# A second PSUM place for attention scores, a larger share of TensorE for early experts, and a new pace in the tail

## The chip, the cores and the metric

The kernel runs on one core of one Trainium2 chip. TensorE multiplies matrices, VectorE (DVE in the profile), ScalarE (ACT) and GpSimd (POOL) work on vectors, and SyncE (SP) issues most transfers. [...] The metric is the device time of one execution in microseconds. Before the change three executions took 15310.87 us at the median (15308.61 to 15326.58).

## The reference

Two layers work on x of 4 images, 3072 tokens each, 256 features, all in fp32.

Layer 0 is group normalization, a Mamba block along one axis, another along the other axis, and a residual. Layer 1 is attention and then experts:

```python
h = tanh(q[:, :, None, :] + k[:, None, :, :] + bh)     # additive attention, 32 hidden units
e = einsum('biju,u->bij', h, Wa[:, 0]) + ba[0]
v = einsum('bij,bjd->bid', softmax(e), inputs)
...
e = leaky_relu(a_src[src] + a_dst[dst])                # graph attention over 1048576 edges
...                                                    # gates of 4 experts, the best 2 kept
out += g * (gelu(x @ W1[e] + b1[e]) @ W2[e] + b2[e])
```

So every pair of tokens of an image needs 32 tanh values. The gates come from sums over edges: edges are sorted, the table rows of sources and destinations are gathered, and their weighted values are added up by destination. The output of an expert doesn't depend on its gate, so it can be computed before the gates are known and kept in HBM. This kernel does so.

## The kernel before, in words

One program holds everything, and its authors wrote the order of the instructions of TensorE, ScalarE, VectorE and GpSimd out by hand: Python generators yield in turn, and what is called first stands first in each engine's queue. [...]

**Layer 0 with attention beside it** (class Layer0, class Attention). Attention of image b runs while Layer0 works on the following images. When Layer0 has ended, attention of the last image is left. The change acts there and in what follows.

**The last attention** (Attention.units, L776). A unit is 32 queries against all 3072 keys. It takes eight tanh instructions on ScalarE, each 128x3072 (th, L815), and each is followed two iterations later by its scores on TensorE: eight products (16 records in the profile, as each fp32 product shows as two) into the PSUM tile pe (L788). pe is 128 x 2 x 512 fp32. There is one place for it (PE_BUFS = 1). After the eighth scores VectorE takes the maximum of each row (nb, L877), and ScalarE the exponentials (pr, L884), both from pe. Then pr is transposed (ptw, L891), copied (pT, L893) and multiplied with the values (pv, L900). The next unit's first scores overwrite pe, so they wait for pr. In the kernel before they are held back over one yield, so that other TensorE work stands ahead of them:

```python
if k == 0:
    pe = self.ps_e.tile([P, 2, JB], F32, tag="pe", name="pe")
    held = behind.pop(0)
else:
    scores(pe, k, behind.pop(0))
```

**Work beside it** (steps, in whole, L1966). Each call of units advances steps once for VectorE and once for TensorE. VectorE's part is the sorting of edges (Edges.sort): compaction with many element-wise instructions, and then one-hot rows (L1219) whose products count edges on TensorE (L1233). For TensorE there is a credit us_t: each th adds SLOT_US and takes off what the attention's own steps need (0.7, 0.4 and 2.9 us a unit, and 1.8 for every fourth). A group of one-hot products costs 8 x PRODUCT_US; what is left goes to early experts.

**Early experts** (Experts.early, L1644). A unit is here a block of 512 tokens with one expert. Its hidden layer is eight products of 128x512 into ph (L1632), two for each of four results, taken out by VectorE with the bias (L1671). Two units then share one visit of ScalarE for GELU (L1676), which needs a table load there and back. The outputs (L1640, into po) are taken out by VectorE (L1683) and kept in HBM. ph has two banks in this phase, po one. 22 units are done so; others were done beside layer 0; 37 are left.

**The tail** (tail, L1730). It counts in steps, three to a remaining expert unit. Each unit computes hidden results, GELU on ScalarE straight from ph (L1714) and outputs. Between them stand the graph's parts: GpSimd issues 540 indirect gathers of table rows (gs, L1337, and the rest of gd, L1052), 16 for a batch of 12 columns up to the 27th of the 36 batches, 12 for the later ones, at most four batches ahead. VectorE scores a batch and builds one-hot tiles (L1374, L1378), and TensorE adds it up (pa, L1388). Batch m is scored at step G0 + PART*m//2. RATE gathers are credited after each of six points of a unit, and a small instruction of GpSimd (pace, L1047) that reads the tile just made ties them to that point. h1 has two buffers, so GELU of a unit waits for the pace instructions of the unit two before it. When a quarter of the graph is done, its gates follow (finish), and then the kept outputs of its six blocks are fetched, weighted and added (L1717) and stored.

PSUM results of the tail come from two pools each (bank, L1594): one counter is shared by ph and po and its parity chooses the pool.

Of the kernel before, what the change touches and what calls it, by code (L numbers as in the profile page):

```python
# [17 lines left out]
F32 = mybir.dt.float32  # L18
# [6 lines left out]
PSUM = bass.MemoryType.PSUM  # L25

P = 128
# [21 lines left out]
TH_BUFS, PE_BUFS, PV_BUFS = 3, 1, 1  # L49
JB = 512  # L50
# [9 lines left out]
G1, K1 = 8, 4  # L60
GP, GG = 12, 4
EDGE_US = 2.4
FIRST, RATE = 14, 2.75
G0, PART = 10, 6
KO_BUFS = 2
SLOT_US, PRODUCT_US = 1.2, 0.11
EU, EG = 32, 2
TB = 512
NQ, FC, NBLK_X = TB // P, FF // P, M // TB
# [570 lines left out]
class Attention:  # L640
# [4 lines left out]
    def __init__(self, ctx, tc, ident, a, x1, x2, xn2T, tab_s, tab_a):  # L645
        self.nc = nc = tc.nc
        self.ident, self.x1, self.x2, self.xn2T = ident, x1, x2, xn2T
        self.tab_s, self.tab_a = tab_s, tab_a
        pool = lambda name, bufs, **k: ctx.enter_context(
            tc.tile_pool(name=name, bufs=bufs, side="right", **k))  # L650
        const = self.const = pool("atc", 1)
        self.rows, self.th, self.wk = pool("atr", 2), pool("atb", TH_BUFS), pool("atw", 1)
        self.ps_e = pool("ate", PE_BUFS, space=PSUM)
        self.ps_v = pool("atv", PV_BUFS, space=PSUM)

        def load(name, shape, ap):
            t = const.tile(shape, F32, tag=name, name=name)
            nc.sync.dma_start(t, ap)
            return t

        self.wt = load("wt_rep", [P, KC, P], a["wt_rep"].rearrange("(k p) m -> p k m", p=P))
        self.wx = load("wx_rep", [P, KC, P], a["wx_rep"].rearrange("(k p) m -> p k m", p=P))
        self.bh = load("bh_rep", [P, 1], a["bh_rep"])
        self.wa = load("wa_blk", [P, P // (4 * R_ATT), QU], a["wa_blk"])
        self.ba = load("ba_rep", [P, 1], a["ba_rep"])
        self.wg = load("wg", [P, KC, HF], a["W_gat"].rearrange("(k p) f -> p k f", p=P))
        self.asr = load("as_rep", [P, HF], a["as_rep"])
        self.adr = load("ad_rep", [P, HF], a["ad_rep"])
        self.eps = const.tile([P, 1], F32, tag="eps1", name="eps1")
        nc.vector.memset(self.eps, 1e-5)  # L670

        self.sel = const.tile([P, QU], F32, tag="sel", name="sel")
        nc.vector.tensor_tensor(self.sel, ident[:, :QU], ident[:, QU:2 * QU], ALU.add)
        for q in range(2, P // QU):
            nc.vector.tensor_tensor(self.sel, self.sel, ident[:, q * QU:(q + 1) * QU], ALU.add)
        self.state = [{} for _ in range(B)]

        self.krep, self.qsel = ([const.tile([P, n], F32, tag=f"{k}{i}", name=f"{k}{i}") for i in range(2)]
                                for k, n in (("krep", TOK), ("qsel", TOK // R_ATT)))
        self.extra, self.entry, self.col, self.asked, self.normed = 0.0, 0, 0, 0, 0  # L680

        self.later, self.now = [], None
# [93 lines left out]
    def units(self, side):  # L776


        nc = self.nc
        todo, behind = [], []  # L780
        NK = QU // R_ATT
        PER = TOK // R_ATT

        def scores(pe, k, th):
            for j in range(2):
                for q in range(NQT):
                    c0 = q * KQ + j * KQ // 2
                    nc.tensor.matmul(pe[q * QU:(q + 1) * QU, j, :KQ // 2], self.wa[:, k, :],  # L788
                                     th[:, c0:c0 + KQ // 2], start=(k == 0), stop=(k == NK - 1))

        def beside():
            while side:
                try:
                    return next(side[0])
                except StopIteration:
                    side.pop(0)

        i = 0  # L800
        while i < B * PER + LAG or todo or self.later:
            b, col = self.entry, self.col = divmod(i, PER)
            if b < B and "krep" not in self.state[b]:

                yield
                late, self.later = self.later, []
                for f in late:
                    f()
                yield
                beside()  # L810
                continue
            if b < B:
                s = self.state[b]
                th = self.th.tile([P, TOK], F32, tag="th", name="th")
                nc.scalar.activation(th, s["krep"], AF.Tanh, bias=s["qsel"][:, col:col + 1])  # L815
                behind.append(th)
                self.now = th
            else:
                self.now = None
            yield  # L820
            late, self.later = self.later, []
            for f in late:
                f()
            busy = tail = held = None
            if behind and i >= LAG:
                n, k = divmod(i - LAG, NK)
                if k == 0:

                    pe = self.ps_e.tile([P, 2, JB], F32, tag="pe", name="pe")
                    held = behind.pop(0)  # L830
                else:
                    scores(pe, k, behind.pop(0))
                if k == NK - 1:
                    tail = self.unit_tail(*divmod(n, TOK // QU), pe)
                    busy = True

            self.extra = 0.0 if tail or not todo else getattr(todo[0], "us", 0.0)
            yield
            if held:
                scores(pe, 0, held)  # L840
            if tail:

                for f in todo:
                    f()
                todo = tail()
            elif todo and hasattr(todo[0], "us"):
                if not todo[0].full:
                    beside()
                todo.pop(0)()
                busy = True  # L850
            elif todo:
                todo.pop(0)()

            if b < B and col == LAG + 3:
                self.load_values(b)
            if b < B and LAG + 4 <= col < LAG + 10:
                self.normalize_values(b, col - LAG - 4)
            if b and col == LAG + 10:
                side.append(self.after(b - 1, *AFTER[-1]))
            side += [self.after(b, t0, t1) for t0, t1 in AFTER[:-1]  # L860
                     if b < B and col == t1 * P // R_ATT + LAG + 10]
            if busy is None:
                beside()
            i += 1
        side.append(self.after(B - 1, *AFTER[-1]))
# [606 lines left out]
class Beside:  # L1472
# [91 lines left out]
    def bank(self):  # L1564
        return self.l0.ps_x.tile([P, 2, self.half], F32, tag="ex", name="ex")
# [7 lines left out]
class Experts:  # L1573
# [3 lines left out]
    def __init__(self, ctx, tc, x2, xn2T, gates, out, dram, beside=None):  # L1577
        self.nc, self.tc, self.dram = tc.nc, tc, dram
        self.x2, self.xn2T, self.gates, self.out = x2, xn2T, gates, out
        pool = lambda name, bufs, **k: ctx.enter_context(tc.tile_pool(name=name, bufs=bufs, **k))  # L1580
        self.xp, self.hp = pool("fx", 2), pool("fh", 2)
        self.ps_h, self.ps_o = [pool("fp", 2, space=PSUM)], [pool("fo", 1, space=PSUM)]
        self.kept, self.done = (beside.kept, beside.units()) if beside else ({}, [])
        self.xts, self.turn = {}, 0

    def open(self, ctx, w):

        pool = lambda name, bufs, **k: ctx.enter_context(self.tc.tile_pool(name=name, bufs=bufs, **k))
        self.w = w
        self.io = pool("fi", 2)  # L1590
        self.ps_h.append(pool("fp2", 2, space=PSUM))
        self.ps_o.append(pool("fo2", 1, space=PSUM))

    def bank(self, pools, shape, tag):  # L1594
        self.turn += 1
        return pools[self.turn % len(pools)].tile(shape, F32, tag=tag, name=tag)

    @staticmethod
    def weights(pool, nc, a):
# [341 lines left out]
def whole(tc, a, dram, out):  # L1941
# [11 lines left out]
    with ExitStack() as ctx:  # L1953
        actx, lctx, ectx = ExitStack(), ExitStack(), ExitStack()
        with tc.manual_schedule(engines={E.PE, E.Activation, E.DVE, E.Pool}):
# [4 lines left out]
            att = Attention(actx, tc, ident, a, x1, x2, xn2T, tab_s, tab_a)  # L1960
            l0.lead_psum = lambda: att.ps_e.tile([P, 2, JB], F32, tag="pe", name="py")[:, 0, :T]
            l0.beside = Beside(lctx, tc, a, l0, att, xn2T, dram)
            side = []
            late = {}

            def steps():  # L1966

                for done in l0.run():
# [3 lines left out]
                        side.append(att.keys(done))  # L1972
                    yield
                lctx.close()
                keep = ctx.enter_context(tc.tile_pool(name="late", bufs=1))
                late["gates"] = keep.tile([P, NH, NEXP], F32, tag="gates", name="gates")
                ed = late["ed"] = Edges(ctx, tc, a, tab_a)
# [6 lines left out]
                while True:  # L1984
                    us_v = min(us_v, 0.0) + EDGE_US
                    while lists and us_v > 0 and len(ed.todo) < 2:
                        us = next(lists, None)
                        if us is None:
                            lists = None
                            pool = ectx.enter_context(tc.tile_pool(name="late2", bufs=1))  # L1990
# [18 lines left out]
                    yield  # L2009

            flow = steps()
            while not side:
                next(flow)
# [19 lines left out]
        n = most.tile([P, 1], I32, tag="n1", name="n1")  # L2033
# [76 lines left out]
```

## Time and profile before

| What | Value |
|---|---|
| median of three executions | 15310.87 us |
| the profiled execution, its time | 15328.57 us |
| its span, first to last instruction | 15326.8 us |
| TensorE / VectorE / ScalarE / GpSimd busy | 77 / 72 / 79 / 59% |
| transfers of the first edge lists are issued (e, L1135) | 11413.9 us |
| first hidden product of an early expert | 11849.1 us |
| first one-hot product | 12471.5 us |
| last tanh starts | 14201.7 us |
| first GELU of the tail | 14271.4 us |
| last gather | 15164.2 us |
| last scatter product (pa) of the tail | 15244 us |

All times inside a profile count from the first instruction. Busy shares are means over stages that have different limits, so the prediction reads each stage by itself. In lists of waits a line reads: engine and instruction that waited, what ended the wait, total us, times, longest.

### The profile page before, as it was taken

What the parts mean: (1) busy time and instruction counts of PE and PEld (TensorE: products, weight loads), DVE (VectorE), ACT (ScalarE), POOL (GpSimd) and SP (SyncE); (2) the same over time, 40 slices, a digit from 0 to 9 for tenths busy, and PEclk for the clock granted to TensorE, in tenths of its full rate; (3) what the DMA queues carried; (4) which work ended last, traced back from release to release, by engine and by line L of the source; (5) the groups of instructions that cost most, each with busy time, mean ns of one, the idle gap of its engine ahead of it and who ended that gap; (6) DMA issues with size and microseconds to landing.
All of it is one profiled execution on the core that took longest, in us unless ns stands there. A gap on an engine that the chain in (4) does not pass through costs nothing. (4 is left out here: it accounts for less than half of the span.)

```text
span 15326.8 us, 225317 instructions
## 1 busy us (share of the span) xinstructions
PE 11744.9 (77%) x86496; PEld 5137.0 (34%) x86496; DVE 11006.6 (72%) x15895; ACT 12153.9 (79%) x9327; POOL 8997.6 (59%) x6935
## 2 busy tenths in 40 slices
PE   5666764777777767788887777888876778988997
PEld 2222332222222233333333333333332334433554
DVE  7888888777777887777777877577778864321367
ACT  3443334999999979999999899999997889999221
POOL 4555556777777767767767677477750024400684
PEclk8888887888888888989998889999988989999998
DMA  5666665445445444454454444355531000010234
GB/s 192 204 203 200 198 204 167 149 148 156 152 150 151 158 156 148 150 152 151 151 150 156 147 149 152 110 156 151 154 127 37 24 13 13 10 31 22 66 95 138
DMA packets 1209121, 2007.93 MB, mean 131 GB/s; under 512 B 412384, under 2 KB 655712, under 8 KB 1204960
## 3 DMA queue, kind: packets, MB, share of 16 engines
q1 hardware_dynamic: 1180384, 1988.07, 41.6%
q0 software_dynamic: 27648, 5.36, 0.8%
q8 instruction: 680, 11.14, 0.3%
q14 instruction: 409, 3.35, 0.1%
HBM read 1875.19 MB, written 117.83 MB: 130 GB/s over the span
## 5 line engine op out<-in xcount | busy, mean ns | idle before, releaser
L815 ACT ACTIVATE th<-krep,qsel 128x3072 f32<-128x3072 f32 x3072 | 8661.7, 2848 | 411.1 <-PE pe L788 392.0
L788 PE MATMUL pe<-th,wa_blk 128*32 128x384 f32 x49152 | 4999.3, 535 | 1196.7 <-ACT pr L884 957.3
L409 POOL TENSOR_TENSOR h<-h,bC 128x768 f32<-128x768 f32 x2048 | 3756.2, 1834 | 3000.4 <-DVE h L402 2634.4
L402 DVE TENSOR_TENSOR_SCAN h<-dA,dB 128x384 f32<-128x384 f32 x4096 | 3687.3, 942 | 1109.4 <-ACT dA L385 752.9
L788 PEld LDWEIGHTS pe<-th,wa_blk 128*32 128x32 f32 x49152 | 1448.0, 116 | 3775.6 <-issue 1992.1
L393 DVE TENSOR_TENSOR dB<-bB,dtu 128x768 f32<-128x768 f32 x2048 | 1942.3, 948 | 123.3 <-DMA bB<-bc 91.2
L385 ACT ACTIVATE dA<-dt,t_A 128x380 f32<-128x380 f32 x2048 | 1127.1, 571 | 887.6 <-DVE h L402 883.1
L385 ACT ACTIVATE dA<-dt,d_A 128x372 f32<-128x372 f32 x2048 | 1102.9, 562 | 601.3 <-DVE h L402 595.9
L428 PE MATMUL py<-h,ident 128*128 128x384 f32 x2176 | 1010.1, 597 | 679.6 <-POOL h L409 678.2
L416 POOL TENSOR_TENSOR h<-h 128x768 f32<-128x768 f32 x752 | 1423.0, 1892 | 53.6
L900 PE MATMUL pv<-xn,pT 128*32 128x257 f32 x18432 | 1116.1, 391 | 172.3 <-DVE pT L893 171.4
L959 POOL TENSOR_SCALAR sf<-sel,f 128x32 f32<-128x32 f32 x384 | 148.6, 410 | 1641.6 <-ACT f L955 1533.9
L893 DVE COPY pT<-ptw 128x512 f32<-128x512 f32 (+1 forms) x768 | 419.0, 546 | 703.7 <-PE ptw L891 703.0
L428 PEld LDWEIGHTS py<-h,ident 128*128 128x128 f32 x2176 | 445.4, 223 | 1247.6 <-POOL h L409 1015.2
L900 PEld LDWEIGHTS pv<-xn,pT 128*32 128x32 f32 x18432 | 583.5, 112 | 759.7 <-DVE pT L893 317.4
L417 POOL TENSOR_TENSOR h<-h 128x384 f32<-128x384 f32 x752 | 783.7, 1042 | 59.0
L418 POOL TENSOR_TENSOR y<-y,h 128x384 f32<-128x384 f32 x752 | 779.9, 1037 | 59.0
L1714 ACT ACTIVATE h<-ph,b 128x512 f32<-128x512 f32 x148 | 96.7, 685 | 662.9 <-POOL pace L1047 473.9
L1337 POOL DMA_INDIRECT gs<-tab_s,si x432 | 526.6, 1219 | 131.3 <-issue 98.8
L891 PE MATMUL ptw<-ident,pr 128*128 128x128 f32 x2304 | 484.7, 328 | 143.5 <-DVE pT L893 79.6
L902 DVE COPY pvs<-pv 128x257 f32<-128x257 f32 x384 | 160.2, 417 | 569.0 <-PE pv L900 568.8
L1052 POOL DMA_INDIRECT gd<-tab_a,di x432 | 467.2, 1082 | 140.6 <-issue 133.4
(302 smaller groups left out, 15311.0 us busy)
## 6 DMA issues: line engine op xcount, KB each, us to landing
bB<-bc SPq DMA_DIRECT2D x2048, 384.0 KB
bC<-bc SPq DMA_DIRECT2D x2048, 384.0 KB
all<-kept SPq DMA_DIRECT2D x24, 2048.0 KB
x<-x SPq DMA_DIRECT2D x144, 256.0 KB
kept<-ko SPq DMA_DIRECT2D x59, 512.0 KB
x<-x SPq DMA_DIRECT2D x192, 128.0 KB
xt<-xn2T SPq DMA_DIRECT2D x41, 512.0 KB
qsel<-xn2T SPq DMA_DIRECT2D x75, 256.0 KB
```

The costliest lines, as they stand in the source:

```text
L385: nc.scalar.activation(inner(dA[:, :T]), inner(blk["dt"][:, e, :]), AF.Exp, scale=blk["w"]["A"][:, e, i + s:i + s + 1])
L393: nc.vector.tensor_tensor(dB, blk["bB"].pop(j), z["dtu"].unsqueeze(1).to_broadcast([P, SB, T]), ALU.mult)
L402: nc.vector.tensor_tensor_scan(h[:, s, :], z.pop(("dA", e, i + s))[:, :T], z["dB"][:, s, :], 0.0, ALU.mult, ALU.add)
L409: nc.gpsimd.tensor_tensor(h, h, blk["bC"].pop(j), ALU.mult)
L416: nc.gpsimd.tensor_tensor(h0, h0, h1, ALU.add)
L417: nc.gpsimd.tensor_tensor(h0[:, 0, :], h0[:, 0, :], h0[:, 1, :], ALU.add)
L418: nc.gpsimd.tensor_tensor(y[e], y[e], h0[:, 0, :], ALU.add)
L428: nc.tensor.matmul(z["py"], self.ident, h[:, s, :], start=(i == 0), stop=(i == DS - 1))
L788: nc.tensor.matmul(pe[q * QU:(q + 1) * QU, j, :KQ // 2], self.wa[:, k, :], th[:, c0:c0 + KQ // 2], start=(k == 0), stop=(k == NK - 1))
L815: nc.scalar.activation(th, s["krep"], AF.Tanh, bias=s["qsel"][:, col:col + 1])
L900: nc.tensor.matmul(pv[q * QU:(q + 1) * QU, :C + 1], pT[:, i, q * QU:(q + 1) * QU], s["xn"][:, q * NK + i, :], start=(i == 0), stop=(i == N ...
L1337: nc.gpsimd.indirect_dma_start(out=gs[:, u, :], out_offset=None, in_=rows, in_offset=bass.IndirectOffsetOnAxis(ap=ed.si[:, q, c0 + u:c0 + ...
```

## The change

It has four parts.

1. When layer 0 has ended, a second pool with one place for pe is opened. While it is there, the unit's number chooses between the two, by n // NK % 2 (NK is 8), and the first scores are no longer held back over the yield.
2. SLOT_US goes from 1.2 to 1.35.
3. PSUM of the experts: ph has one bank before the tail instead of two, and three more in the tail; ph and po count their turns apart, so that each goes round its banks.
4. In the tail PART goes from 6 to 5 and RATE from 2.75 to 3.2: a batch every 2.5 steps, which is 0.83 units, and 6.4 gathers a step.

```diff
-FIRST, RATE = 14, 2.75
-G0, PART = 10, 6
+FIRST, RATE = 14, 3.2
+G0, PART = 10, 5
 KO_BUFS = 2
-SLOT_US, PRODUCT_US = 1.2, 0.11
+SLOT_US, PRODUCT_US = 1.35, 0.11
...
-        self.ps_e = pool("ate", PE_BUFS, space=PSUM)
+        self.ps_e, self.ps_e2 = pool("ate", PE_BUFS, space=PSUM), None
...
                 n, k = divmod(i - LAG, NK)
                 if k == 0:
-
-                    pe = self.ps_e.tile([P, 2, JB], F32, tag="pe", name="pe")
+                    places = self.ps_e2 if self.ps_e2 and n // NK % 2 else self.ps_e
+                    pe = places.tile([P, 2, JB], F32, tag="pe", name="pe")
+                if k == 0 and not self.ps_e2:
+
                     held = behind.pop(0)
                 else:
                     scores(pe, k, behind.pop(0))
...
-        self.ps_h, self.ps_o = [pool("fp", 2, space=PSUM)], [pool("fo", 1, space=PSUM)]
+        self.ps_h, self.ps_o = [pool("fp", 1, space=PSUM)], [pool("fo", 1, space=PSUM)]
...
-        self.xts, self.turn = {}, 0
+        self.xts, self.turn = {}, {}
...
-        self.ps_h.append(pool("fp2", 2, space=PSUM))
+        self.ps_h += [pool("fp2", 3, space=PSUM)] * 3
...
-        self.turn += 1
-        return pools[self.turn % len(pools)].tile(shape, F32, tag=tag, name=tag)
+        self.turn[tag] = self.turn.get(tag, -1) + 1
+        return pools[self.turn[tag] % len(pools)].tile(shape, F32, tag=tag, name=tag)
...
                 lctx.close()
+                att.ps_e2 = actx.enter_context(
+                    tc.tile_pool(name="ate2", bufs=1, side="right", space=PSUM))
```

## The prediction

> **What bounds the kernel now.** I read the page's 40 slices first, to see where the changed code lies.
>
> ```profile
> PE   5666764777777767788887777888876778988997
> ...
> ACT  3443334999999979999999899999997889999221
> POOL 4555556777777767767767677477750024400684
> ```
>
> The slices up to about the 30th are layer 0 with attention beside it, which the diff leaves alone. In slices 30 to 37 ACT (ScalarE) climbs back to nine tenths: the last attention. Then ACT falls to two and POOL (GpSimd) rises to eight: the tail. Next I asked for busy time by stage: sort alone (A), sort with early experts (B), one-hot products (C), rest of attention (D), tail up to the last gather. Columns: stretch and length, then busy us and instructions of PE, PEld, DVE, ACT, POOL; clock; DMA.
>
> ```profile
> 11425.00:11790.00 365.00, 241.71 (x2212) 100.92 (x2212) 302.49 (x451) 261.19 (x108) 5.74 (x13) 0.83 0.14 40
> 11790.00:12470.00 680.00, 512.24 (x4560) 204.11 (x4560) 604.41 (x998) 554.93 (x230) 21.60 (x24) 0.89 0.08 23
> 12470.00:13620.00 1150.00, 1032.10 (x11017) 489.11 (x11014) 434.95 (x838) 1122.79 (x461) 468.12 (x692) 0.95 0.08 15
> 13620.00:14206.00 586.00, 508.83 (x4845) 215.49 (x4843) 110.46 (x216) 571.45 (x239) 8.20 (x24) 0.95 0.08 25
> ...
> 14245.00:15165.00 920.00, 850.29 (x2530) 492.09 (x2530) 541.14 (x950) 207.93 (x264) 755.74 (x750) 0.96 0.35 91
> ```
>
> In A and B DVE is at 83 and 89%, and ACT idles 28 and 18% of the time. In C and D ACT is at 97.6%. There PE has little to spare: busy 1541 of 1736 us, and the waits (C and D together, engine by engine) fill the rest:
>
> ```profile
> ACT th L815 <- PE pe L788: 35.1, 59, 3.2
> ```
> ```profile
> PE pe L788 <- ACT pr L884: 153.8, 58, 10.7
> ...
> PE pe L788 <- ACT th L815: 10.4, 11, 2.6
> ```
>
> One unit boundary in time, from the timeline, shows what that 153.8 us is:
>
> ```profile
> 12637.55 1.50 PE L788 MATMUL pe<-th,wa_blk 128*32 128x384 f32 x16
> ...
> 12638.98 0.89 PE L1233 MATMUL pc<-hot_go 128*128 128x96 bf16 x8
> 12639.11 0.96 DVE L877 TENSOR_REDUCE nb<-pe 128x1 f32<-128x768 f32 x1 [0.30 <-PE pe L788]
> ...
> 12639.69 1.06 PE L1632 MATMUL ph<-xt,krep 128*128 128x512 f32 x2
> ...
> 12642.15 0.88 ACT L884 ACTIVATE pr<-pe,nb 128x768 f32<-128x768 f32 x1
> ...
> 12643.08 2.79 PE L788 MATMUL pe<-th,wa_blk 128*32 128x384 f32 x16 [2.33 <-ACT pr L884]
> ```
>
> The eighth scores end at 12639.0. DVE needs 0.96 us for the maximum, ACT finishes its tanh (2.08 us more), then pr takes 0.88, and only then may the next scores overwrite pe. PE covers part with a product and a hidden matmul, then waits 2.33 us.
>
> In the tail POOL never stops: 31 gathers and 11 paces per 50 us. ACT waits for it, in units 26.3 us apart on average:
>
> ```profile
> ACT h L1714 <- POOL pace L1047: 465.0, 25, 24.0
> ...
> POOL gs L1337 <- issue: 94.2, 371, 0.4
> ```
> ```profile
> 14394.40 1.27 ACT L1714 ACTIVATE h<-ph,b 128x512 f32<-128x512 f32 x2 [20.91 <-POOL pace L1047]
> ...
> 14421.92 1.27 ACT L1714 ACTIVATE h<-ph,b 128x512 f32<-128x512 f32 x2 [22.12 <-POOL pace L1047]
> ```
>
> From 15025 on ACT waits for PE ph instead and units are 23.4 us apart: there PE is the bound. After the last unit (15213) DVE sets the end.
>
> [...] sixteen score records take 1.50 us, and 2.79 after a 2.33 us wait. [...]
>
> **The change, part by part.**
>
> *Alternating places.* The place is chosen by n // NK % 2, with n the unit's number and NK = 8 th to a unit. It therefore changes every eighth unit, not every unit: at 13 of the 104 boundaries after the second place opens. The other 91 wait for pr as before. Waits for pr were 84.5 us in A (11 times), 72.9 in B (17), 92.5 in C (38), 61.4 in D (20): 7.7, 4.3, 2.4, 3.1 each. Removed: one in A (8 us of PE; I take −5 of time, as DVE at 83% follows), about 2.6 in B (11 us), 9 in C and D (23 us).
>
> *Scores moved ahead.* With a second place, scores of k = 0 are no longer held over the yield. In the instruction order, early-expert and product work between the eighth and the next first scores falls from 1.6 to 1.2 us a unit (priced at 1.0 us a hidden product, 0.48 an output product, 0.9 a group of eight one-hot products), and 0.65 now stands behind the wait. What is queued behind the waiting first scores is PE's whole queue: that work, then ptw. Cover lost: 0.4 us for 19 units in B (8 us) and 62 in C and D (25 us).
>
> *SLOT_US 1.35.* Early units go from 22 to 29, the tail's from 37 to 30. Early and product PE work rises from 112 to 139 us in B, from 269 to 319 in C, from 125 to 154 in D: +27, +50, +29. ACT gets 7 GELUs of 1.90 us and eight more table loads of 1.283: 13.3 + 10.3 = 24 us, nearly all in C and D, where ACT is the bound. Four more GELU visits in C and D make PE wait longer at a boundary: the five long waits there (10.5, 3.0, 4.3, 9.3, 10.7) average 7.6 against 2.3, so 4 × 5.3 = 21 us.
>
> *One hidden bank.* The next hidden product must now wait for DVE's bias add, which stands just ahead of it in the order and behind sort pieces. With two banks the trace shows no such wait, so I bound it: 0 if DVE is always there first; 2.9 us as for po, which has one bank (25.7 us, 9 times in B). In the first units the add would have come 1.2, 2.4 and 1.1 us late. About 38 results in B at 1.2, half lost in DVE's own lateness: 23 us. 68 in C and D at 0.45: 30 us (ends 0 and 110 for both).
>
> *B together:* 27 + 8 + 23 − 11 = 47; PE there has no slack (busy plus waits are 680), but 76 us of DVE idle let some be caught up: **+40**, between 0 and +80. *C and D:* 50 + 29 + 25 + 30 + 21 − 23 = 132 of PE time. Slack: pr starts on average 1.7 us after the maximum, because ACT is inside a tanh; 69 units × 1.7 = 116 us PE can lose before pr moves. 132 − 116 = 16, ACT's own floor is 19 to 24, and unevenly spread slack adds: **+35**, between +15 and +90.
>
> *Tail.* PE loses 7 units × 15.0 us (hidden 253.6 us for 546 records, 16 to a unit: 7.4; output 270.0 for 1136, 32 to a unit: 7.6) = 105 us. POOL keeps all 540 gathers, at 1.18 + 0.25 = 1.44 us, and 33 paces of 0.5 us go: −16. RATE and PART only make it 6.4 gathers a step in place of 5.5. A unit with 19.2 gathers and 6 paces needs 30.6 us of POOL, while PE needs 25.5 (23.4 and a fifth more of pa, 383.6 us in 36 batches). So the last gather comes about 15150, the last unit about 15169 (before 15213): −44. But then more is left: 4 batches of 10.8 us DVE work in place of 2.2, and 5.5 blocks of 7.8 us in place of 2.5, since the third quarter's gates come late against 30 units. 151 us stand against 106, which took 114: **−8**, between −45 and +20. The second po bank saves waits of 28 us that POOL's pace hides; without that cover they would count.
>
> *Sum:* −5 + 40 + 35 − 8 = +62. The profiled execution took 15328.6 us (span 15326.8), 17.7 above the median of 15310.9. 15328.6 + 62 − 17.7 = **15373 us**.
>
> **Rivals.**
> 1. *Hidden in the wait* (not slower). All extra PE work fits into the pr waits, and DVE's adds are in time. Place: B to D; price: B +5, C and D ACT's +23, A −5, tail −15: +8, so 15319. It decides if the single bank costs under 0.2 us a result. For: 227 us of pr waits in B to D. Against: in B pr follows the maximum by 0.2 us (waits for GELU apart), so there is no slack.
> 2. *The tail is PE's.* If PE sets the tail, its 105 us go, and the 28 us of po waits, while the drain grows by 37: −96 in place of −8; with my attention 15285, with rival 1's about 15238. It decides if a gather costs POOL under 1.1 us. For: PE is at 92% there. Against: 465 us of ACT waiting for POOL.
> 3. *Single bank worse.* 2.9 us each in B[...]: +150, so 15461. For: po's own waits. Against: DVE is at 38% in C and 19% in D.
>
> That the places alternate unit by unit, giving back most of the 311 us of PE waits, would be a fourth; the index excludes it.
>
> **How the numbers follow.** Main case 0.52 (15335 to 15430), rival 1 0.17, rival 2 0.19, rival 3 0.12. A measurement can tell about 0.2% (31 us) from no change. Faster: rival 2 and a little of rival 1, 0.20. Within: most of rival 1, 0.13. Slower: 0.67. The range leaves out half of rival 2 and most of rival 3: 15240 to 15460.
>
> **What would show it.** After: PE waits for pr still some 80 to 100 times past 11425, with 7 of 8 boundaries waiting; a new wait of ph for DVE h L1671 worth 30 to 80 us; end of attention (last th) 50 to 90 us later than 14205; tail from last th to end within 45 us of 1125; 30 units there at 30 to 31 us apart while POOL binds. Wrong if pr waits nearly vanish, if the last th ends by 14220, or if units in the tail come every 25 us.

## The result

The changed kernel took 15344.58 us at the median (15328.66 to 15366.21, 17 runs), the kernel before 15316.14 us (15299.16 to 15326.75, 17 runs). The ratio is 1.0019, with a 95% interval of 1.0012 to 1.0026: some 28 us slower. The forecast was 62 us slower.

The profiled execution has a span of 15344.1 us. Busy time by stage, at the edges used before (stretch and length; then PE, PEld, DVE, ACT, POOL busy us and instructions; clock; DMA share and GB/s). Lines from L829 on stand two or more further down than before, so L1634 here is L1632 there:

```profile
11425.00:11790.00 365.00, 235.96 (x2248) 98.71 (x2248) 312.21 (x467) 270.59 (x112) 5.73 (x13) 0.87 0.13 40
11790.00:12470.00 680.00, 523.87 (x4576) 217.57 (x4580) 593.55 (x977) 544.18 (x225) 14.33 (x22) 0.92 0.08 24
12470.00:13620.00 1150.00, 1049.94 (x11124) 509.65 (x11120) 447.72 (x860) 1125.89 (x465) 464.02 (x694) 0.97 0.09 20
13620.00:14206.00 586.00, 518.44 (x4800) 224.66 (x4792) 116.58 (x224) 568.80 (x239) 8.17 (x24) 0.97 0.08 25
...
14245.00:15165.00 920.00, 812.25 (x2369) 459.94 (x2368) 530.48 (x932) 192.79 (x243) 726.90 (x705) 0.94 0.31 80
```

PE does more in the third and fourth stretch (1568 us in place of 1541) and less in the tail (812 for 850), as it should. ACT has hardly moved (1694.7 us in those two stretches for 1694.2). PE's waits over the whole of the last attention, 11425 to 14230, are these (what waited, for what: total us, times, longest):

```profile
PE pe L788 <- ACT pr L886: 199.9, 61, 20.6
PE ph L1634 <- DVE h L1673: 81.6, 52, 7.1
PE po L1642 <- DVE ko L1685: 28.7, 19, 3.3
```

In the kernel before the same question, 11425 to 14206, gives:

```profile
PE pe L788 <- ACT pr L884: 311.3, 86, 20.2
```

So the wait for pr is still the largest, though it lost 111 us. The hidden product's wait for VectorE's bias add, 82 us, wasn't there before. Yet the span grew by 17 us, so these sums don't say where time went. That is read from marks that both traces share: the end of layer 0 (its last h on POOL, L409), the 93rd pr from the end (the first hidden product of an early expert stands some 40 us ahead of it), the 69th pr from the end (the first one-hot product stands some 100 us ahead of it), and the last tanh.

| Stretch | Before | After | Change | Forecast |
|---|---|---|---|---|
| layer 0's end to 93rd last pr (A) | 503.2 | 497.6 | −5.6 | −5 |
| to 69th last pr (B) | 686.5 | 703.5 | +17.0 | +40 |
| to the last tanh (C and D) | 1631.8 | 1650.2 | +18.4 | +35 |
| last tanh to the end (tail) | 1125.1 | 1117.1 | −8.0 | −8 |

The sum is +21.8 us; layer 0 itself ended 4.5 us sooner in this execution, which leaves the 17.3 us between the two spans. Layer 0's end lies anywhere from 11363 to 11389 in the profiles of this study, with no cause in any diff, so from here on stretches are compared, and whole times by their ratios.

### The profile page after: what moved, and what is told of

It is laid out like the page before. It is cut to its first block, busy times and chain, and to the rows that moved or that the text cites. A ratio compares the mean times of both kernels' runs of the same rounds, so it can differ in the third digit from the quotient of the medians.

```text
span 15344.1 us, 225269 instructions
## 1 busy us (share of the span) xinstructions
PE 11725.3 (76%) x86496; PEld 5126.0 (33%) x86496; DVE 11026.6 (72%) x15923; ACT 12152.6 (79%) x9311; POOL 8965.7 (58%) x6902
## 5 line engine op out<-in xcount | busy, mean ns | idle before, releaser
L409 POOL TENSOR_TENSOR h<-h,bC 128x768 f32<-128x768 f32 x2048 | 3753.7, 1833 | 3004.2 <-DVE h L402 2645.6
L1339 POOL DMA_INDIRECT gs<-tab_s,si x432 | 503.2, 1165 | 139.7 <-issue 107.8
L879 DVE TENSOR_REDUCE nb<-pe 128x1 f32<-128x768 f32 x384 | 362.0, 943 | 291.1 <-PE pe L788 291.0
```

The costliest lines, as they stand in the source:

```text
L409: nc.gpsimd.tensor_tensor(h, h, blk["bC"].pop(j), ALU.mult)
L1339: nc.gpsimd.indirect_dma_start(out=gs[:, u, :], out_offset=None, in_=rows, in_offset=bass.IndirectOffsetOnAxis(ap=ed.si[:, q, c0 + u:c0 + ...
```

## Experiments on the attention

Four runs took apart what the change does to the attention; two more followed from them. Stretches are in us, as in the table; "attention" is from layer 0's end to the last tanh. Ratios are to the kernel before, measured beside each.

| Run | B | C and D | Attention | Tail | Ratio (95%) |
|---|---|---|---|---|---|
| before | 686.5 | 1631.8 | 2821.5 | 1125.1 | 1 |
| changed | 703.5 | 1650.2 | 2851.3 | 1117.1 | 1.0019 (1.0012–1.0026) |
| e1_alt | 696.2 | 1621.6 | 2811.7 | 1117.3 | 0.9989 (0.9983–0.9996) |
| e2_one_place | 713.2 | 1653.5 | 2873.5 | 1111.6 | 1.0028 (1.0016–1.0039) |
| e3_one_place_two_banks | 698.4 | 1633.5 | 2832.5 | 1106.4 | 0.9997 (0.9988–1.0005) |
| e4_hold | 703.6 | 1650.2 | 2861.0 | 1110.3 | 1.0019 (1.0010–1.0028) |
| e14_shared | 692.3 | 1647.2 | 2834.3 | 1103.2 | 0.9997 (0.9989–1.0006) |
| e9_alt_shared | 685.6 | 1612.3 | 2787.3 | 1099.1 | 0.9970 (0.9957–0.9982) |

How far such stretches repeat can be seen where two runs have the same attention. The attention of before gave 1631.8 and 1632.4 us in C and D in two further runs, that of the change 1650.5 in another: within 1 us. B gave 688.5 and 691.0 for before, but 710.7 for the change. A and B together repeat to some 6 us in the attention of before, to 17 in that of the change, and to 3 or 4 in those of e1_alt and e9_alt_shared, with two or three profiles of each.

### Alternating by unit: e1_alt

```diff
-                    places = self.ps_e2 if self.ps_e2 and n // NK % 2 else self.ps_e
+                    places = self.ps_e2 if self.ps_e2 and n % 2 else self.ps_e
```

> The changed kernel with one edit: the place of the scores is chosen by n % 2, so that it changes with every unit. Theory of the prediction (the index lets 7 of 8 boundaries wait as before): waits of the first scores for pr, 200 us past 11425 in the changed kernel, fall below 40 us. ACT idles 94, 136, 24 and 17 us in the four stages of the attention there, so the last tanh can come 40 to 90 us earlier than 14227, and the time is 15255 to 15305. Rival (the wait only moves): PE gets stuck on pv, ptw, ph and po waiting for DVE instead, the last tanh stays within 15 us of 14227 and the time within 15 us of 15344.

Measured: 15304.87 us, some 40 us below the change; the last tanh at 14186.9, 40 us sooner. The same waits of PE, 11425 to 14230:

```profile
PE ph L1634 <- DVE h L1673: 92.6, 56, 7.0
PE ptw L893 <- ACT pr L886: 71.1, 37, 7.7
PE pe L788 <- ACT th L815: 47.9, 53, 5.5
...
PE pe L788 <- ACT pr L886: 20.7, 1, 20.7
```

Of 61 waits of scores for pr one is left, in A, of 20.7 us. The index is settled: with n // NK the places don't alternate where it counts. One boundary in time, from the timeline of this run:

```profile
12630.72 2.79 PE L788 MATMUL pe<-th,wa_blk 128*32 128x384 f32 x32
12632.29 0.96 DVE L879 TENSOR_REDUCE nb<-pe 128x1 f32<-128x768 f32 x1 [2.05 <-PE pe L788]
12633.44 0.88 PE L1235 MATMUL pc<-hot_keep 128*128 128x96 bf16 x8
12633.81 0.88 ACT L886 ACTIVATE pr<-pe,nb 128x768 f32<-128x768 f32 x1
...
12634.74 0.66 PE L893 MATMUL ptw<-ident,pr 128*128 128x128 f32 x4 [0.42 <-ACT pr L886]
12635.33 1.50 PE L788 MATMUL pe<-th,wa_blk 128*32 128x384 f32 x16
```

The 32 records are the last scores of one unit and the first of the next in one go; the wait of 2.33 us that the prediction showed here is gone, and 0.42 us at the transpose of pr is left. Both theories had a part: 179 us less of these waits brought 40 us of attention (57 against the second profile of the change's attention), in part because waits for pr at the transpose (71 us, 11 before the edit) and for the next tanh (48, 24 before) took their place. ACT is nearly full, as the stretch 12470 to 13620 of this run shows:

```profile
12470.00:13620.00 1150.00, 1061.57 (x11266) 516.55 (x11262) 446.79 (x858) 1138.36 (x471) 468.27 (x686) 0.98 0.09 20
```

ACT is busy 99% of it. Where PE still waits for ACT, it waits for ACT's work (71.1 us for pr at the transpose, 47.9 for th), and only once, for the 20.7 us in A, for ACT to free a buffer; the largest wait is now that for VectorE's bias add (93 us).

### What every eighth unit is worth: e2_one_place

```diff
-                    places = self.ps_e2 if self.ps_e2 and n // NK % 2 else self.ps_e
+                    places = self.ps_e
```

> The changed kernel with the second place opened but never taken; scores still not held back. Theory of the prediction: the 13 boundaries that alternate save 7.7 us each in the sort, 4.3 beside it and 2.5 later, so waits for pr rise from 200 to some 240 us, and the last tanh comes 10 to 25 us later than 14227: 15354 to 15369. Rival (what alternates every eighth unit is worth nothing, the slack before pr takes it): last tanh within 8 us of 14227, time within 10 us of 15344.

Measured: 15359.75 us; last tanh 14237.0, 10 us later than in the changed kernel's profile, though layer 0 had ended 12 us sooner. Waits for pr, where the changed kernel has 199.9 us in 61:

```profile
PE pe L788 <- ACT pr L886: 217.0, 71, 10.3
```

C and D are 3.3 us longer than in the changed kernel, B 9.7, A 9. The sign is that of the theory, but the intervals of the two ratios overlap, and only the 3.3 us lie outside what repeats. The 13 boundaries are worth little.

### Scores held back: e4_hold

```diff
-                if k == 0 and not self.ps_e2:
+                if k == 0:
```

> The changed kernel with the first scores of a unit held back over the yield again, all else as changed. Theory of the prediction: 0.4 us of cover a unit come back, 33 us of PE time, of which half shows: last tanh 10 to 20 us earlier than 14227, time 15322 to 15337. Rival (what stands ahead of the scores or behind them makes no difference, since the queue as a whole isn't shorter): last tanh within 8 us of 14227, time within 10 us of 15344.

Measured: 15354.34 us, last tanh at 14230.6. C and D took 1650.2 us, as in the changed kernel to a tenth, and B 703.6 against 703.5; A was 507.2, against 497.6 and 507.1 in the two profiles of the change. The waits for pr did fall, from 200 to 173 us, and those of ph for VectorE rose. The rival is right: moving 0.4 us of work from behind the waiting scores to ahead of them moves the wait and no time. What stood behind waiting scores waited too: in the kernel before, the one-hot rows hot_move were finished at 12636.57 us, and their products came only at 12648.08, though PE was idle from 12640.75 to 12643.08, until pr was done.

### Two hidden banks: e3_one_place_two_banks and e14_shared

The first goes back to one place for the scores and two hidden banks, with the scores held back as before; of the change it keeps SLOT_US 1.35, the separate turns and the tail's pace.

```diff
-                att.ps_e2 = actx.enter_context(
-                    tc.tile_pool(name="ate2", bufs=1, side="right", space=PSUM))
...
-        self.ps_h, self.ps_o = [pool("fp", 1, space=PSUM)], [pool("fo", 1, space=PSUM)]
+        self.ps_h, self.ps_o = [pool("fp", 2, space=PSUM)], [pool("fo", 1, space=PSUM)]
...
-        self.ps_h += [pool("fp2", 3, space=PSUM)] * 3
+        self.ps_h.append(pool("fp2", 2, space=PSUM))
```

> The changed kernel with the scores as before (one place, first scores held over the yield) and the hidden results in two banks before the tail (two more in the tail): what stays is SLOT_US 1.35, the separate turns and the tail's pace. Theory of the prediction: the wait of ph for DVE's bias add (83 us) goes, 29 us of time from the single bank and the lost cover go with it, while the alternation's gain is lost too: last tanh 10 to 35 us earlier than 14227, time 15310 to 15335. Rival (the wait for ph only stood in front of the wait for pr): waits for pr rise by as much as ph's fall, 280 us or more, last tanh within 10 us of 14227, time within 12 us of 15344.

Measured: 15312.58 us, last tanh at 14208.9, as the theory had it. The seven more early units, with all their products, GELUs and table loads, cost 11.0 us of attention against before: some 9 in A and B, 1.7 in C and D. That is the price of SLOT_US (with the separate turns, which stay in). Waits for pr, though nothing alternates here:

```profile
PE pe L788 <- ACT pr L886: 237.5, 81, 20.0
```

How C and D took the work shows in busy times between the marks, 69th pr from the end to last tanh, of before:

```profile
12569.89:14201.67 1631.78, 1449.39 (x14894) 660.16 (x14894) 511.22 (x992) 1591.52 (x657) 427.49 (x644) 0.95 0.08 18
```

of this run:

```profile
12575.40:14208.89 1633.49, 1485.54 (x15108) 691.44 (x15108) 526.36 (x1015) 1606.22 (x667) 430.03 (x644) 0.97 0.09 23
```

and of the changed kernel:

```profile
12576.78:14227.03 1650.25, 1493.67 (x15108) 696.28 (x15112) 527.45 (x1015) 1608.59 (x667) 422.49 (x644) 0.97 0.09 22
```

ACT is busy 15 us more than before in this run and 17 us more in the changed kernel. Its idle time was 40 us before; it is 27 here and 42 in the changed kernel.

The second keeps the changed kernel's places and gives ph and po a pool of two banks that they share. Both use tiles of 128x512 fp32 (po as 128 x 2 x 256), so the pools ask for no more PSUM than in the changed kernel.

```diff
-        self.ps_h, self.ps_o = [pool("fp", 1, space=PSUM)], [pool("fo", 1, space=PSUM)]
+        both = self.both = pool("fp", 2, space=PSUM)
+        self.ps_h, self.ps_o = [both], [both]
...
-        self.ps_h += [pool("fp2", 3, space=PSUM)] * 3
-        self.ps_o.append(pool("fo2", 1, space=PSUM))
+        self.ps_h = [pool("fp2", 4, space=PSUM)]
...
+        place = pools[self.turn[tag] % len(pools)]
+        return place.tile(shape, F32, tag="pb" if place is self.both else tag, name=tag)
```

> The changed kernel with one edit: ph and po of the early experts take turns in one pool of two banks before the tail (in the tail ph has four banks and po these two); the places still change every eighth unit. Theory (the single hidden bank is what the change pays for its second place; from layer 0's end to the last tanh one place with two banks took 2833 us, the changed kernel 2851 and 2868 in two profiles): waits of ph for DVE's h, 83 us past 11425, fall below 20, that stretch takes 2825 to 2840 us, and with a tail of 1099 to 1117 the time is 15300 to 15328. Rival (the waits for pr take it up where the places don't alternate: 240 us or more of them): the stretch stays at 2850 or more and the time at 15335 or more.

Measured: 15315.01 us, so the change without its single bank is level with before. Attention 2834.3 us, within the expected 2825 to 2840. In its waits both halves of the expectation came true, the rival's too:

```profile
PE pe L788 <- ACT pr L886: 259.1, 81, 19.8
```

Waits of ph for h fell from 82 to 7 us and waits for pr rose by 59, and the time fell nevertheless, by some 30 us: 17 to 34 of attention, against the two profiles of the change's, and 7 to 14 of tail. The sum of these two waits fell by 16 us only, so it does not measure the time here.

Where the bank counts is B: 692.3 against 703.5 and 710.7. In C and D it gave only 3.0 us, and holding the scores back gave 0.0; yet e3_one_place_two_banks, with two banks and held scores, is 16.7 us shorter there than the change, 14 of it in ACT's idle time. Either both have to be undone together, or the place of po, which has a bank to itself in that run, matters. No run tells these apart, and it stays open.

### Both cures: e9_alt_shared

The edits of e1_alt and e14_shared together.

> The run with places by n % 2, and besides it ph and po of the early experts take turns in one pool of two banks, so that neither has a single bank; in the tail ph has four banks of its own and po these two. Theory (a single hidden bank costs 28 us of the attention, as one place with two banks against one place with one bank showed): waits of ph for DVE's h, 93 us past 11425 with n % 2, fall below 20, and the last tanh comes 8 to 22 us earlier than 14187, the less since ACT is at 99% there; time 15283 to 15298. Rival (ACT is full, so PE's waits are free once the places alternate): last tanh within 5 us of 14187, time within 6 us of 15305.

Measured: 15264.37 us, better than expected. The last tanh came at 14176.4, but layer 0 had ended 13.8 us later than in e1_alt's profile, so the attention is 24.4 us shorter: 9.3 of it in C and D, 10.6 in B. Though ACT was at 99%, there was room. The expectation compared last tanhs alone, and left out the tail, which is 18 us shorter here than in e1_alt. Of that, 8 us lie ahead of the first gather of gs, which starts 38 us after the last tanh in place of 46, and 7 between the first and the last. Whether ph's four banks of its own did this was not tried by itself.

## Experiments on the tail

### The pace constants: e5_tail_only and e6b_old_pace

The kernel before with the new constants, and the changed kernel with the old ones. The edit of the first:

```diff
-FIRST, RATE = 14, 2.75
-G0, PART = 10, 6
+FIRST, RATE = 14, 3.2
+G0, PART = 10, 5
```

The second has the same lines the other way round, and one more edit, since with these constants a batch itself can ask for the last gathers:

```diff
             while j not in gr.got:
-                next(gathers)
+                next(gathers, None)
```

Without it (e6_old_pace) the list of gathers runs out before the program is complete, and there is no result.

> The kernel before with the tail's pace alone changed: PART 5 and RATE 3.2; 37 units are left and all else is as before. Theory of the prediction (POOL never pauses, so a pace moves no gather; the tail of the changed kernel is shorter because seven units are gone): units cost POOL 30.6 us for 28 units, then nine are left for PE at 15 to 17 us; the last unit comes near 15250, the drain after it is short; the tail from the last tanh to the end stays within 15 us of 1125 and the time within 15 us of 15317. Rival (the pace is what shortened the tail): tail 1105 or less, time 15300 or less.

Measured: 15326.37 us, ratio 1.0007 (1.0000 to 1.0014), tail 1130.4 us. The last 48 output records on TensorE, the last unit's 32 among them, began at 15251.1, as expected.

> The changed kernel with PART 6 and RATE 2.75 in the tail, as before, on its 30 units; what the units leave of the gathers is issued when their batch asks for them. Theory of the prediction (POOL never pauses, the pace moves no gather): the units end earlier, 27 us apart, the last batches follow them; last gather within 15 us of 957 us after the last tanh, and time within 20 us of 15344. Rival (the pace is what matters, since batch 35 then stands at step 115 where the units have 90): the tail grows from 1117 by 40 us or more, time 15385 or more.

Measured: 15349.23 us, ratio 1.0015 (1.0008 to 1.0022), tail 1110.7 us; the last gather came 978 us after the last tanh, 21 us later than in the changed kernel (957), 6 more than expected, and what follows it took 133 us in place of 160. PART and RATE change nothing in time that shows: the new ones make the tail 5.3 us longer with 37 units and 6.4 with 30, within what tails of one program differ by (e1_alt, e2_one_place and e4_hold have the changed kernel's tail: 1110 to 1117). Seven units fewer are worth 13 to 20 us, together with the tail's new banks, which were not tried alone.

### Without the pace: e10_alt_no_pace and e13_before_no_pace

Gathers are bound to their points no longer. On top of e1_alt, and on the kernel before:

```diff
-            if credit[0] >= 1:
-                ed.behind(t)
```

> The run with places by n % 2, and besides it no pace instruction in the tail: gathers follow each other, held only by their buffers. Theory of the prediction (POOL sets the tail): 176 paces of 0.32 us and 0.17 of issue, 88 us, leave POOL, and GELU no longer waits for them; the last gather comes 60 to 90 us sooner after the last tanh than 956 us, PE becomes the bound at 25 us a unit, and the tail falls from 1117 to between 1045 and 1080: time 15235 to 15270. Rival (the tail is PE's and DVE's, the pace only a line in the queue): tail within 15 us of 1117, time within 15 us of 15305.

Measured: 15229.36 us, ratio 0.9945 (0.9931 to 0.9959). The tail is 1038.6 us, 79 less than in e1_alt and below the expected 1045 to 1080. What ACT waits for from 14280 on, first in the changed kernel:

```profile
ACT h L1716 <- POOL pace L1049: 395.7, 26, 27.5
...
ACT h L1716 <- PE ph L1634: 65.9, 17, 16.0
```

and then without the pace:

```profile
ACT h L1716 <- PE ph L1634: 293.1, 61, 15.5
```

POOL held the units up, and released, PE does. Gathers of gs from 14150 on, changed kernel and then this run (ns min/median/max, first and last start):

```profile
L1339 POOL DMA_INDIRECT gs<-tab_s,si x432: 940/985/2972, 14273.4 to 15184.2; - x144
```

```profile
L1339 POOL DMA_INDIRECT gs<-tab_s,si x432: 940/945/2915, 14235.2 to 15071.0; - x144
```

The last gather comes 882 us after the last tanh in place of 957. From it to the end it takes 157 us here and 160 in the changed kernel: the last batch, its gates, and the blocks that wait for them. So the tail is shorter by what the last gather moved. That distance is not fixed: with other constants or more units it is 133 us (e6b_old_pace) to 181 (e5_tail_only).

> The kernel before with no pace instruction in its tail, 37 units, PART 6 and RATE 2.75. Theory (POOL's pace bound the tail before, PE stood close behind): PE needs some 25 us a unit, so the last unit comes about 985 us after the last tanh in place of 1011, and the tail falls from 1125 to between 1075 and 1110; against 1038 with 30 units, seven units are then worth 40 to 70 us where PE binds. Rival (POOL's gathers alone set both tails, units are free): 1050 or less. Second rival (PE set the tail before): 1115 to 1135.

Measured: 15306.03 us, ratio 0.9986 (0.9979 to 0.9993), tail 1115.7 us, 9 less than with the pace. That is 6 us outside what was expected, at the edge of the second rival. With 37 units PE stands right behind POOL:

```profile
ACT h L1714 <- PE ph L1632: 516.8, 111, 23.4
```

And here the gathers have to wait for VectorE to use up earlier ones, as the batches are tied to the steps of the units:

```profile
POOL gs L1337 <- DVE v L1276: 63.9, 8, 16.4
```

Without the pace 37 units take 77 us more than 30 (1115.7 against 1038.6, the latter with PART 5, RATE 3.2 and the new banks, whose shares weren't measured; PE waits only 1 us for po's bank in the former from 14280 on); with it, 13 to 20. The fewer units that the change leaves in the tail are worth something only once POOL is out of their way.

## The best version, and one step too far

> Places by n % 2, ph and po in a common pool of two banks before the tail, and no pace in the tail: the two edits that helped, together. If they are apart, as their places are (attention and tail), the attention is as in the run with the common pool (34 us shorter than before, from layer 0's end to the last tanh) and the tail as in the run without pace (1038 us against 1125): time 15185 to 15210. Rival (the shorter tail of the common pool, 1099 against 1117, was only its four hidden banks easing POOL's pace, or the two edits share one gain): 15215 or more.

Measured (e11_alt_shared_no_pace): 15208.68 us, ratio 0.9924 (0.9908 to 0.9941): 116 us faster than before. The attention was 2790.5 us with C and D at 1612.3, as in e9_alt_shared; the tail took 1045.3. The gains add, as their places are apart; the 18 us by which the common pool's tail was shorter don't come on top. In that the rival was right, though not in its time of 15215 or more.

With still more early units:

```diff
-SLOT_US, PRODUCT_US = 1.35, 0.11
+SLOT_US, PRODUCT_US = 1.5, 0.11
...
-FIRST, RATE = 14, 3.2
-G0, PART = 10, 5
+FIRST, RATE = 14, 4.0
+G0, PART = 10, 4
```

The edit of e6b_old_pace, `next(gathers, None)`, is in here too.

> The combination (places by n % 2, common pool of two banks, no pace) with still more early units: SLOT_US 1.5, and PART 4 and RATE 4.0 so that the batches fit the fewer units. Theory (without pace POOL's 540 gathers of 1.42 us, 767 us, are the tail's next floor, PE being at 93 to 97%): the tail shortens from 1038 by at most 25 us, the attention grows by 5 to 20 us since ACT is at 99% there and gets seven more GELUs and their table loads; time within 20 us of the combination with 1.35. Rival (PE sets the tail once the pace is gone): seven units of 15 us less, tail 960 or less, time 60 us or more below the combination with 1.35.

Measured (e12_slot15): 15279.81 us, ratio 0.9970 (0.9958 to 0.9983), some 70 us worse than with 1.35, which neither theory had. C and D grew by 32 us to 1644.2. Busy times between their marks, with 1.35:

```profile
12548.30:14160.64 1612.34, 1483.28 (x15094) 693.96 (x15094) 528.79 (x1015) 1602.05 (x667) 430.74 (x644) 0.98 0.09 23
```

and with 1.5:

```profile
12546.46:14190.71 1644.25, 1543.21 (x15348) 741.40 (x15345) 546.74 (x1042) 1622.70 (x680) 431.37 (x644) 0.98 0.10 25
```

ACT idled 10 us with 1.35, so its 21 us of further work are paid in full, and it idles 11 us more besides. PE is at 94% there, so it may set part of the time; no run tells. The tail took 1073.4 us, 28 more, though it had 24 units in place of 30. Its gathers:

```profile
L1339 POOL DMA_INDIRECT gs<-tab_s,si x432: 941/947/2739, 14228.1 to 15070.1; - x144
```

The last comes 879 us after the last tanh, as with 30 units (882 and 886): from the first gather to the last it is 836 to 848 us in these three runs, with 24 units as with 30, where 767 was expected. But 194 us follow it in place of 157 to 160. More kept blocks wait for the last gates: 232 weighted additions of 0.48 us come after the last gather, against 176, which is 27 us of the 34 to 37. Which share PART and RATE have in that wasn't measured.

## Why the prediction was right or wrong

*The index* was read rightly. The places alternate every eighth unit; 61 boundaries still wait, where the forecast had 80 to 100. The waits fell by 111 us, where alternation was to take some 40. Its own share is 17 us in 10 waits (e2_one_place against the change). Another 59 are gone because the wait for ph stands in front of them and PE comes later to the scores: with two hidden banks 259 us in 81 waits are left (e14_shared). The rest isn't split, but much of it needs no alternation: e3_one_place_two_banks, with one place, has 238 us left (holding the scores back takes 27 of these waits by itself in e4_hold).

*A, −5*: measured −5.6, but A repeats only to some 10 us.

*B, +40*: measured +17 and, in a second profile of the same attention, +24. The step that failed is "PE there has no slack". SLOT_US was put at 27 of B. PE's busy time in B did rise by 28 us in e3_one_place_two_banks (532 to 560), but its idle time fell by 16 (154 to 139), and B grew by 12. So the waits that were counted as full were slack in part. The single bank was put at 23 and measured 11 to 18 (e14_shared against the two profiles). The cover lost was put at 8 and cost nothing (e4_hold).

*C and D, +35*: measured +18.4. "ACT's own floor is 19 to 24" failed. Five of the seven GELUs and six of the eight table loads fell here, the rest in B, and ACT's busy time rose by 15 us in e3_one_place_two_banks, but C and D grew by 1.7 us there: ACT had idled 40 us of the stretch before, and 13 of these took up the work. Of the 25 us of lost cover nothing showed on its own. What is left, 16.7 us, is the bank and the order of the scores together, or po's own bank; which it is stays open. It is less than the 30 + 25 that were put in before slack. That 132 − 116 = 16 comes near the 18.4 by itself is luck, as the 25 in it cost nothing.

*Tail, −8*: measured −8.0. That it agrees to the tenth is luck, as tails of the same program lie between 1110 and 1117. The mechanism held: POOL keeps its 540 gathers, and what goes are 33 paces. They were put at 16 us; from the first gather to the last it took 7 us less (911 for 918). The GELUs of the 30 units span 847 us, 28 a unit, where 30 to 31 were forecast while POOL binds. The two terms were both too small and cancelled. The last 16 output records start 62.6 us sooner after the last tanh (941.6 against 1004.2; forecast 44), and the drain behind them is 54.5 us longer (175.4 against 120.9; forecast 37). The 37 sets an estimate of 151 against a measured 114; against the estimate for before, 106, it would have been 45, and the tail's forecast about 0. The plainer reading would have been that the end stands some 160 us behind the last gather in both, and that gather moved 5 us.

*The rivals.* "Hidden in the wait" was half right: SLOT_US is nearly hidden, the single bank isn't. "The tail is PE's" was wrong for this kernel, but its price was near: where the pace was gone, seven units fewer, with the new constants and banks, were worth 77 us, where it had 96. "Single bank worse" was wrong: the wait for ph was 82 us, just above the 30 to 80 expected, but it cost some 17 to 34 us of time. Of its 150 us, 110 are 38 results at 2.9 in B; the other 40 were the author's estimate. No run shows that a second place for the scores makes a single hidden bank necessary, and e14_shared does without one: there ph and po take turns in the two banks that they had one each.

*The sum.* The direction held, and of the mechanism the index, the new wait for the hidden bank and POOL's hold on the tail; the size was 62 for 28. The mis-sized terms are B's and C and D's, each about twice too large. The last tanh came 25 us later (14227.0 against 14201.7), where 50 to 90 was expected.

## What to carry to other kernels

Check by its index that a double buffer turns at every use: turning every eighth time, it kept its price (the hidden bank given up with it, 17 to 34 us of attention) and lost nearly all its gain. Two users with one bank each, of the same size, can take turns in one pool: here that made the time some 30 us shorter. And before more work is moved out of a stage, ask whether the engine that paces the stage does any of that work: here GpSimd did not, and its own small ordering instructions were worth more (79 us) than seven units of TensorE as long as they were there (13 to 20).

## What the runs showed that was not expected

- C and D repeat to 1 us between executions and between kernels with the same attention (1621.6 and 1621.6; 1612.3 and 1612.3; 1650.2 and 1650.5), while A and B of the changed kernel's attention differed by 17 us in two profiles, and layer 0's end by up to 26 us over all of them.
- With a second bank in turn, PE's waits for a hidden bank fell from 82 to 7 us and those for pr rose by 59, while the attention became 17 to 34 us shorter.
- 176 pace instructions on POOL cost 79 us of the tail with 30 units, 0.45 us each. In the changed kernel's profile they take 0.32 us at the median and 0.61 on average. With 37 units 209 of them cost 9 us, as PE stood right behind POOL: without them ACT waits 516.8 us for PE (e13_before_no_pace).
- Scores that followed a long wait took longer. In the attention of before, sixteen score records took 1.50 us at the median after a wait under 1 us; after each of the 20 waits over 5 us they took 2.79, and after waits of 2 to 3 us anything from 1.50 to 2.79.
